# A graph layer on one TensorE: the product of scores and v by one level of Strassen's algorithm

## The chip, the cores and the metric

The kernel runs on one core of one Trainium2 chip. Time is device microseconds of one launch. The median of three runs of the kernel before is 1751.72 us (1751.53 to 1753.11).

## The reference, cut to what matters

64 matrices x of 256 tokens by 512 features go through two layers with one shared 256 by 256 adjacency matrix. All is fp32.

```python
# layer 0
h = relu(layernorm(x))
q, k, v = h @ Wq.T, h @ Wk.T, h @ Wv.T
rel = adj.T * (q @ k.T)                       # 256 x 256 scores, masked
rel = rel / norm(rel, axis=2)                 # each row by its length
x = x + rel @ v                               # <- the product that the change touches
# layer 1
h = relu(layernorm(x))
x = x + (adj @ h) @ weight + bias
```

## The kernel before, in words

The batch is worked in 32 pairs of two matrices (`NB = 2`), each of two token blocks of 128. `x` of five pairs stays in SBUF in a ring (`x_ring`), and each pair's result is added into it in place before it is written out.

For one pair, in steady state, `steady` (L670) issues these stages; each engine runs them in exactly the order in which the Python code issues them, since everything is under `manual_schedule`:

- **attend(i)** (L408): rel times v. Four output tiles of 128 by 512, each two matmuls with 512 moving columns into a PSUM bank of its own; VectorE adds each tile into x, and takes the layer-1 statistics of that tile right after (`side`).
- **project_v(i+1)** (L327): h times Wv.
- **scores(i+1)** (L340): g times h, where g = h times (Wq, Wk folded into one matrix).
- **gather(i)** (L458): adj times h of layer 1, taken in two fp32r parts (upper and lower) when adj is exact in few bits, which it is here (`exact`).
- **project_g(i+2)** (L309): h times the folded matrix.
- **mix(i)** (L481): the gathered rows times weight, added into x.

project_v, scores, project_g and mix already use one level of Strassen's algorithm in Winograd's form. `winograd` (L169) runs seven products instead of eight over three PSUM banks: `bank_a` holds products 1, 6, 7, 4 one on top of the other, `bank_c` products 5 and 3, `bank_b` product 2. After each product a "take" reads the bank and adds it to its quarter of the result. A later product that adds into a bank waits until the take before it has read the bank. In V, scores and g, a take that is the first for its quarter is a copy on ScalarE; the others are adds on VectorE. The first factors of the seven products come from `left_operands` (L152, four sums), the second from `right_operands` (L126, four differences); they are made on VectorE.

`winograd`'s argument `side` is a table from the number of the product (its slot, 0 to 6) to pieces of work that are issued right after that product's take. All other work is placed through it by hand: `norm`'s statistics (`chunk`, L240), its `root` (a small VectorE step and ScalarE's square root) and `end` (reciprocal and bias), the `relus`; for layer 1 `relu_bias` (L439: relu on ScalarE, then the bias added to x by GpSimd), `upper` (a cast on ScalarE) and `lower` (a difference on VectorE). Relus of layer 1 go through two buffers (tag `h2c`), so the third one waits for the first `lower`.

The scores are turned with DMAs (`place`, L376) and four VectorE transposes (`turn`, L383, `turned`), which stand in slot 5 of mix before. The same slot has the end of the layer-0 norm of pair i+4 and its four relus.

Of the kernel before, what the change touches and what calls it, by code (L numbers as in the profile page):

```python
# [19 lines left out]
def kernel(  # L20
# [57 lines left out]
    small = ctx.enter_context(tc.tile_pool(name="small", bufs=3))  # L78
    ps_m = ctx.enter_context(tc.tile_pool(name="ps_m", bufs=8, space=bass.MemoryType.PSUM))

    X, H, HL, G, GS, V, R, H2, Y = ({} for _ in range(9))

    ring = [const.tile([P, NB, NC, D], F32, name=f"x_ring{n}") for n in range(5)]
    blocks = const.tile([P, TC, DC, P], F32, name="blocks")
# [63 lines left out]
    def left_blocks(at):  # L148

        return lambda i, j: at[:, j * HC : (j + 1) * HC, i]  # L150

    def left_operands(pool, at, tag, i):  # L152


        s = pool.tile([P, 3, HC, HT_], F32, tag=tag, name=f"{tag}_{i}")
        a = left_blocks(at)
        v = nc.vector
        steps = [
            lambda: v.tensor_sub(s[:, 0], a(0, 0), a(1, 0)),
            lambda: v.tensor_add(a(1, 0), a(1, 0), a(1, 1)),  # L160
            lambda: v.tensor_sub(s[:, 1], a(1, 0), a(0, 0)),
            lambda: v.tensor_sub(s[:, 2], a(0, 1), s[:, 1]),
        ]
        return (
            {1: a(0, 0), 2: a(0, 1), 3: s[:, 2], 4: a(1, 1), 5: a(1, 0), 6: s[:, 1], 7: s[:, 0]},
            steps,
        )

    def winograd(product, take, side={}, early=False):  # L169

# [138 lines left out]
    def project_g(i, side={}):  # L309

        g = work.tile([P, DC, NC, HT_], F32, tag="g", name=f"g_{i}")

        def take(t, k, bank, first):
            dst = g[:, k * HC : (k + 1) * HC, t, :]
            src = bank.rearrange("p (e t) -> p e t", e=HC)
            if first:
                nc.scalar.copy(dst, src)  # L317
            else:
                nc.vector.tensor_add(dst, src, dst)

        winograd(product_tokens_moving(HL[i], m_right), take, side)
        t = work.tile([P, 3, HC, HT_], F32, tag="gt", name=f"gt_{i}")
        G[i], GS[i] = right_operands(
            lambda j, k: g[:, j * HC : (j + 1) * HC, k], [t[:, n] for n in range(3)]
        )

    def project_v(i, side={}, tag="v"):  # L327
        V[i] = work.tile([P, NB, NC, D], F32, tag=tag, name=f"v_{i}")
# [11 lines left out]
    def scores(i, side={}, by_matmul=False):  # L340


        left, right = HL.pop(i), G.pop(i)
        rel = work.tile([P, NB, NC, N], F32, tag="rel", name=f"rel_{i}")
        placed = work.tile([P, NB, NC, NC, P], F32, tag="placed", name=f"placed_{i}")
        turned = work.tile([P, NB, NC, NC, P], F32, tag="turned", name=f"turned_{i}")
        square = work.tile([P, N], F32, tag="square", name=f"square_{i}")
        rn = small.tile([P, NB, NC], F32, tag="rn", name="rn")
        R[i] = turned

        def take(t, k, bank, first):
            dst = rel[:, :, k, ts(t, P)]
            src = bank[:, :HT_].rearrange("p (b m) -> p b m", b=NB)
            if first:
                nc.scalar.copy(dst, src)
            else:
                nc.vector.tensor_add(dst, src, dst)

        def mask(k):
            nc.vector.tensor_mul(  # L360
                rel[:, :, k], rel[:, :, k], adjt_sb[:, k : k + 1, :].to_broadcast([P, NB, N])
            )

        def square_sum(b, k):
            nc.scalar.activation(square, rel[:, b, k], AF.Square, accum_out=rn[:, b, k : k + 1])

        def root():
            nc.scalar.activation(rn, rn, AF.Sqrt)

        def inverse():  # L370
            nc.vector.reciprocal(rn, rn)

        def scale(b, k):
            nc.scalar.activation(rel[:, b, k], rel[:, b, k], AF.Copy, scale=rn[:, b, k : k + 1])

        def place():  # L376
            rv = rel.rearrange("p b k (t m) -> p (b k t) m", m=P)
            pv = placed.rearrange("p b k t n -> p (b k t) n")
            for j in range(P // S):
                for k in range(P // S):  # L380
                    nc.sync.dma_start(out=pv[ts(j, S), :, ts(k, S)], in_=rv[ts(k, S), :, ts(j, S)])

        def turn(b, k):  # L383
            nc.vector.transpose(turned[:, b, :, k], placed[:, b, k])  # L384

        def each(f):
            return [(lambda b=b, k=k: f(b, k)) for k in range(NC) for b in range(NB)]

        def turn_at_once():
            for b in range(NB):  # L390
                pt = ps_m.tile([P, T], F32, tag="pm", name="pr")
                for t in range(NC):
                    for k in range(NC):
                        nc.tensor.transpose(
                            pt[:, ts(t * NC + k, P)], rel[:, b, k, ts(t, P)], ident
                        )
                nc.scalar.copy(turned[:, b].rearrange("p t k n -> p (t k n)"), pt)

        winograd(product_of_tokens(left, right), take, side)
        if by_matmul:  # L400
            masks = [lambda: mask(0), lambda: mask(1)]
            return masks, each(square_sum), root, inverse, rn, turn_at_once
        return (
            [lambda: mask(0), lambda: mask(1)], each(square_sum), root, inverse, each(scale), place,
            each(turn),
        )

    def attend(i, side={}, scale=None):  # L408
        rel, v, xt = R.pop(i), flat(V.pop(i)), flat(X[i])
        for b in range(NB):  # L410
            for n in range(NC):
                c = b * NC + n
                pm = ps_m.tile([P, 512], F32, tag="pm", name="pu")
                for m in range(NC):
                    nc.tensor.matmul(  # L415
                        pm[:, :D], rel[:, b, m, n], v[:, b * NC + m, :],
                        start=(m == 0), stop=(m == NC - 1),
                    )
                if scale is None:
                    nc.vector.tensor_add(xt[:, c, :], pm[:, :D], xt[:, c, :])  # L420
                else:
                    nc.vector.scalar_tensor_tensor(
                        xt[:, c, :], pm[:, :D], scale[:, b, n : n + 1], xt[:, c, :],
                        op0=ALU.mult, op1=ALU.add,
                    )
                run(side.get(c, ()))


    def ln1(i, exact):
# [179 lines left out]
    def first_pairs(exact):  # L609
# [10 lines left out]
        })  # L620
        place_blocks(1)
        turned1, sums1 = transpose_blocks(1)
        gs = GS.pop(0)
        stats, root, end, relus = ln0(2)
        project_v(0, {
            0: gs[0:2], 1: gs[2:3] + stats[0:1], 2: gs[3:4] + stats[1:2], 3: stats[2:3],
# [11 lines left out]
            4: [inverse] + scales + [place] + stats[3:4] + [root], 5: [end] + w_steps[0:1],  # L638
            6: w_steps[1:4],
        })  # L640
        gs = GS.pop(1)
        turned2, sums2 = transpose_blocks(2)
        project_v(1, {
            0: gs[0:2], 1: gs[2:3] + turned2[0:2], 2: gs[3:4] + turned2[2:4] + relus[0:2],
# [11 lines left out]
        if exact:  # L656
# [1 line left out]
        project_g(2, by_slot(layer_1(parts), {  # L658
            1: [inverse], 3: scales + [place], 4: turned3[0:1], 5: turned3[1:2], 6: turned3[2:4],
        }))  # L660
        y_steps = gather(0, exact, {0: turned3[4:6], 1: turned3[6:7], 2: turned3[7:8]})
        run(y_steps[0:2])
        stats, root, end, relus = ln0(4)
        mix(0, {
            0: y_steps[2:3], 1: y_steps[3:4] + stats[0:1], 2: stats[1:2], 3: stats[2:3],
            4: stats[3:4] + [root], 5: [end] + turns + relus, 6: sums3,
        })
        place_blocks(4)

    def steady(i, exact):  # L670


        stats, root, end, relus, uppers, lowers = ln1(i, exact)
        gs = GS.pop(i + 1)
        attend(i, {c: [stats[c]] for c in range(TC)})
        project_v(i + 1, {
            0: [root, gs[0], end, relus[0], relus[1]],
            1: [uppers[0], uppers[1], gs[1], lowers[0]],
            2: [relus[2], lowers[1]],
            3: [relus[3], uppers[2], uppers[3], gs[2]],  # L680
            4: [lowers[2]],
            5: [lowers[3], gs[3]],
        })
        masks, squares, norm_root, inverse, scales, place, turns = scores(i + 1)
        turned, sums = transpose_blocks(i + 3)
        y_steps = gather(i, exact, {
            0: masks + turned[0:1],
# [1 line left out]
            2: squares[2:4] + turned[3:5],  # L689
            3: [norm_root, inverse] + turned[5:8],  # L690
        })
        project_g(i + 2, {
            0: scales + [place] + y_steps[0:1],
            1: y_steps[1:3],
            2: y_steps[3:4] + sums[0:1],
            3: sums[1:2],
            4: sums[2:3],
            5: sums[3:4],
        })
        if i + 4 < NP:  # L700
            stats, root, end, relus = ln0(i + 4)
            mix(i, {n: [stats[n]] for n in range(TC)} | {4: [root], 5: [end] + turns + relus})
            place_blocks(i + 4)
        else:
            mix(i, {5: turns})

    def last_pairs(exact):

        a, b, c = NP - 3, NP - 2, NP - 1
        stats, *parts = ln1(a, exact)  # L710
        gs = GS.pop(b)
        attend(a, {n: [stats[n]] for n in range(TC)})
        project_v(b, by_slot({0: gs[0:1], 1: gs[1:2], 3: gs[2:3], 5: gs[3:4]}, layer_1(parts)))
        masks, squares, norm_root, inverse, scales, place, turns = scores(b)
        y_steps = gather(a, exact, {
            0: masks, 1: squares[0:2], 2: squares[2:4], 3: [norm_root, inverse],
        })
        project_g(c, {0: scales + [place] + y_steps[0:1], 1: y_steps[1:3], 2: y_steps[3:4]})
        gs = GS.pop(c)
        project_v(c, {  # L720
            0: gs[0:1], 1: gs[1:2], 2: gs[2:3], 3: gs[3:4], 5: turns[0:2], 6: turns[2:4],
        }, tag="h")
# [50 lines left out]
```

## Time and profile before

| | busy us | share of the span |
|---|---|---|
| TensorE, matmuls | 1734.2 | 99% |
| TensorE, weight loads | 1447.8 | 83% |
| VectorE | 1216.7 | 69% |
| ScalarE | 644.6 | 37% |
| GpSimd | 199.4 | 11% |

The span of the profiled execution is 1751.9 us and the granted TensorE clock 0.997. One fp32 matmul appears as two records. A steady pair by stages (from the trace, one pair, us from the span's start):

| stage | from | to | us | VectorE busy | ScalarE busy |
|---|---|---|---|---|---|
| attend | 501.57 | 508.76 | 7.19 | 6.24 | 2.46 |
| V | 508.76 | 521.00 | 12.24 | 10.03 | 6.75 |
| scores | 521.00 | 527.25 | 6.25 | 2.26 | 1.70 |
| gather | 527.25 | 530.90 | 3.65 | 2.96 | 2.55 |
| g | 530.90 | 542.98 | 12.08 | 8.28 | 5.12 |
| mix | 542.98 | 555.07 | 12.09 | 7.94 | 1.27 |

How to read it: TensorE's busy time fills the span, so a stage's length is the length of its matmuls plus the moments in which TensorE waits. The last columns say how full the engines beside it are in that stage. Records of matmuls overlap at their ends, so lengths are taken from the start of one group to the start of the next.

### The profile page before, as it was taken

To read this page: it belongs to the slowest core of one execution; us is meant where nothing else is said; L and a number is where in the kernel's file an instruction comes from. 1 tells how busy PE (TensorE), PEld (TensorE's weight loads), DVE (VectorE), ACT (ScalarE), POOL (GpSimd) and SP (SyncE) were. 2 spreads that over 40 slices of the span, in tenths; PEclk is the share of its full clock that TensorE was granted. 3 is DMA by queue.
4 is the path that set the end of the run, shared out by engine and by line. 5 is a ranking of instruction groups with operands and counts; after the bars stand their busy time and mean duration, and the time that the engine had idled before them with its cause. 6 is when DMAs were issued, how large, how long until landed. Compare 5 with 4: busy or idle time off the path is not lost.

```text
span 1751.9 us, 23847 instructions
## 1 busy us (share of the span) xinstructions
PE 1734.2 (99%) x8822; PEld 1447.8 (83%) x8822; DVE 1216.7 (69%) x2353; ACT 644.6 (37%) x1387; POOL 199.4 (11%) x167
## 2 busy tenths in 40 slices
PE   8999999999999999999999999999999999999998
PEld 7978887888888888878888888888788888888886
DVE  6776777666777667776667776677766677766555
ACT  3433433334423334333344233343333442333332
POOL 0011111011110011110111100111101111001111
PEclk9999999999999999999999999999999999999999
DMA  6423333223332233332233422333322333222101
GB/s 232 64 44 70 77 80 71 58 53 84 74 85 55 51 76 76 81 68 61 53 83 74 85 56 52 74 78 80 74 57 52 83 75 85 53 55 50 30 13 69
DMA packets 425966, 122.27 MB, mean 70 GB/s; under 512 B 398064, under 2 KB 399344, under 8 KB 425840
## 3 DMA queue, kind: packets, MB, share of 16 engines
q1 hardware_dynamic: 413248, 80.28, 24.9%
q0 software_dynamic: 8432, 32.51, 5.2%
q10 hardware_dynamic: 4160, 7.87, 1.3%
q8 instruction: 71, 1.16, 0.3%
q14 instruction: 55, 0.45, 0.1%
HBM read 38.27 MB, written 33.55 MB: 41 GB/s over the span
## 4 chain that ended last, share of the span: by engine, by line
PE 95%; DVE 3%; ACT 0%; DMA 0%; issue 0%; ACTq 0%; DVEq 0%
PE bank_a L210 25%; PE bank_a L198 12%; PE bank_c L210 12%; PE pu L415 12%; PE py L470 7%; PE bank_a L222 7%; PE bank_b L210 6%; PE bank_c L198 6%; PE bank_c L222 3%; PE bank_b L198 3%; PE bank_b L222 2%; DVE st L241 1%; DMA wk_sb<-in_L_gnn_Wk_dram 0%; DVE x_ring L420 0%; DVE x_ring L487 0%
## 5 line engine op out<-in xcount | busy, mean ns | idle before, releaser
L415 PE MATMUL pu<-v,turned 128*128 128x512 f32 x512 | 227.1, 596 | 3.2 <-DVE turned L384 0.9
L443 POOL TENSOR_TENSOR x_ring<-x_ring,bias_bc 128x512 f32<-128x512 f32 x128 | 174.6, 1383 | 452.1 <-ACT h2c L253 452.1
L415 PEld LDWEIGHTS pu<-v,turned 128*128 128x128 f32 x512 | 94.7, 190 | 120.8 <-issue 107.2
L241 DVE BATCH_NORM_STATS2 st<-x_ring 128x6 f32<-128x512 f32 x256 | 176.2, 688 | 4.4
L334 ACT COPY v<-bank_a 128x512 f32<-128x512 f32 x96 | 56.0, 583 | 308.3 <-PE bank_a L210 300.9
L451 DVE TENSOR_TENSOR h<-h2c,h 128x512 fp32r<-128x512 f32 x128 | 123.2, 980 | 62.9 <-ACT h L447 62.9
L494 POOL DMA_DIRECT2D out_dram<-x_ring x31 | 24.0, 773 | 1080.3 <-issue 796.7
L487 DVE TENSOR_TENSOR x_ring<-bank_a,x_ring 128x512 f32<-128x512 f32 x128 | 87.3, 682 | 80.3 <-PE bank_a L210 76.4
L317 ACT COPY g<-bank_a 128x512 f32<-128x512 f32 x96 | 56.2, 585 | 213.7 <-PE bank_a L198 213.5
L470 PE MATMUL py<-adjt_r,h 128*128 128x256 f32 x1024 | 124.9, 280 | 0.0
L210 PE MATMUL bank_a<-w_t,ys 128*128 128x256 f32 x512 | 121.3, 380 | 1.8 <-DVE x_ring L487 1.8
L210 PE MATMUL bank_a<-wv_t,hs 128*128 128x256 f32 x512 | 121.0, 379 | 0.0
L198 PE MATMUL bank_a<-hs,m_t 128*128 128x256 f32 x512 | 120.9, 379 | 0.0
L470 PEld LDWEIGHTS py<-adjt_r,h 128*128 128x128 f32 x1024 | 119.4, 188 | 0.1
L246 ACT ACTIVATE rs<-rs 128x4 f32<-128x4 f32 x64 | 13.2, 206 | 268.2 <-DVE rs L245 268.2
L210 PEld LDWEIGHTS bank_a<-w_t,ys 128*128 128x128 f32 x512 | 96.9, 190 | 16.2 <-DVE x_ring L487 3.0
L253 ACT ACTIVATE h<-x_ring,nb,rs 128x512 f32<-128x512 f32 x124 | 90.9, 802 | 50.3 <-DVE nb L250 50.3
L253 ACT ACTIVATE h2c<-x_ring,nb,rs 128x512 f32<-128x512 f32 x128 | 97.4, 807 | 30.9 <-DVE h L451 16.4
L198 PEld LDWEIGHTS bank_a<-hs,m_t 128*128 128x128 f32 x512 | 97.3, 190 | 13.2
L210 PEld LDWEIGHTS bank_a<-wv_t,hs 128*128 128x128 f32 x512 | 97.3, 190 | 13.2
L420 DVE TENSOR_TENSOR x_ring<-pu,x_ring 128x512 f32<-128x512 f32 x124 | 85.6, 690 | 27.3 <-PE pu L415 20.4
L302 DVE STREAM_TRANSPOSE ht<-blocks 128x256 f32<-128x256 f32 x248 | 87.2, 408 | 1.1 <-DMA blocks<-h 1.1
(152 smaller groups left out, 3235.3 us busy)
## 6 DMA issues: line engine op xcount, KB each, us to landing
blocks<-h SPq DMA_DIRECT2D x496, 64.0 KB, 2.3
out_dram<-x_ring POOLq DMA_DIRECT2D x31, 1024.0 KB, 5.2
x_ring<-in_x_dram SPq DMA_DIRECT2D x28, 1024.0 KB, 5.6
placed<-rel SPq DMA_DIRECT2D x496, 32.0 KB, 2.0
x_ring<-in_x_dram ACTq DMA_DIRECT2D x4, 1024.0 KB, 5.4
wq_sb<-in_L_gnn_Wq_dram SPq DMA_DIRECT2D x4, 256.0 KB, 5.1
wk_sb<-in_L_gnn_Wk_dram ACTq DMA_DIRECT2D x4, 256.0 KB, 6.9
wv_sb<-in_L_gnn_Wv_dram ACTq DMA_DIRECT2D x1, 1024.0 KB, 5.4
```

The source lines that it names most:

```text
L198: nc.tensor.matmul(bank[:, e * HT_ : (e + 1) * HT_], right[n][:, d, ts(e, P)], left[n][:, d, :], start=(start and e == 0 and d == 0), stop ...
L210: nc.tensor.matmul(bank[:, b * HD : (b + 1) * HD], left[n][:, d, ts(b, P)], right[n][:, d, :], start=(start and b == 0 and d == 0), stop=( ...
L222: nc.tensor.matmul(bank[:, ts(b, P)], right[n][:, d, ts(b, P)], left[n][:, d, ts(b, P)], start=(start and b == 0 and d == 0), stop=(d == H ...
L241: nc.vector.bn_stats(st[:, c, :], src[:, c, :])
L253: nc.scalar.activation(dst, src[:, c, :], AF.Relu, bias=nb[:, c : c + 1], scale=rs[:, c : c + 1])
L302: nc.vector.transpose(ht[:, d, half].rearrange("p (b n) -> p b n", b=NB), by_half[:, :, half, d])
L415: nc.tensor.matmul(pm[:, :D], rel[:, b, m, n], v[:, b * NC + m, :], start=(m == 0), stop=(m == NC - 1),)
L420: nc.vector.tensor_add(xt[:, c, :], pm[:, :D], xt[:, c, :])
L443: nc.gpsimd.tensor_tensor(xt[:, c, :], xt[:, c, :], bias_bc, ALU.add)
L451: nc.vector.tensor_sub(dst[:, 1, c, :], whole_h[c], dst[:, 0, c, :].bitcast(F32))
L470: nc.tensor.matmul(pm[:, d, :], left[:, b * NC + m, ts(d0 + d, P)], right, start=(n == 0), stop=(n == len(terms) - 1),)
L487: nc.vector.tensor_add(xt[block], bank.rearrange("p (b e) -> p b e", b=NB), xt[block])
```

## The change

In pairs 1 to 29 the product of the normed scores and v is done by seven half-size products instead of eight, to cut TensorE's work. Pairs 0, 30 and 31 keep the plain product.

Per product there are now two matmuls of 256 moving columns, one for each matrix of the pair. The left factors are made in place from `turned`, with the dead `rel` tile for the new sums; the right ones from `v` and a new tile under the tag of g's factors (`gt`). So g's differences are only prepared after attend (`g_operands`), and v's in project_g, slots 4 to 6. The turns move from slot 5 to slot 4 of mix, and the four sums of the turned scores (`rel_steps`) go into slot 5. Each take of the new product is an add into x on VectorE. A quarter of x is finished only at the end of the product, so the statistics of layer 1 move from attend into slots 0 and 1 of V, and what follows from them (root, end, relus, upper and lower parts) moves back by some slots, the last two lower parts into scores. In the first pair the sums for pair 3 still stand in slot 6 of mix.

```diff
+    def attend_operands(i):
+        turned, rel = R.pop(i)
+        v, t = V.pop(i), work.tile([P, 3, NB, HD], F32, tag="gt", name=f"vt_{i}")
+        room = rel.rearrange("p b k m -> p (b k m)")
+        left, left_steps = left_factors(
+            lambda n, m: turned[:, :, m, n],
+            [room[:, ts(j, HT_)].rearrange("p (b n) -> p b n", b=NB) for j in range(3)],
+        )
+        right, right_steps = right_operands(
+            lambda m, k: v[:, :, m, ts(k, HD)], [t[:, n] for n in range(3)]
+        )
+        R[i] = left, right
+        return right_steps, left_steps
+
+    def attend_by_strassen(i):
+        xt, (left, right) = X[i], R.pop(i)
+        def product(bank, n, start):
+            for b in range(NB):
+                nc.tensor.matmul(
+                    bank[:, ts(b, HD)], left[n][:, b], right[n][:, b],
+                    start=(start and b == 0), stop=True, skip_group_check=True,
+                )
+        def take(t, k, bank, first):
+            dst = xt[:, :, t, ts(k, HD)]
+            nc.vector.tensor_add(dst, bank.rearrange("p (b e) -> p b e", b=NB), dst)
+        winograd(product, take)
...
     def steady(i, exact):
-        stats, root, end, relus, uppers, lowers = ln1(i, exact)
-        gs = GS.pop(i + 1)
-        attend(i, {c: [stats[c]] for c in range(TC)})
-        project_v(i + 1, {
-            0: [root, gs[0], end, relus[0], relus[1]],
-            1: [uppers[0], uppers[1], gs[1], lowers[0]],
-            2: [relus[2], lowers[1]],
-            3: [relus[3], uppers[2], uppers[3], gs[2]],
-            4: [lowers[2]],
-            5: [lowers[3], gs[3]],
-        })
-        masks, squares, norm_root, inverse, scales, place, turns = scores(i + 1)
+        attend_by_strassen(i)
+        stats, *parts = ln1(i, exact)
+        gs = g_operands(i + 1)
+        project_v(i + 1, v_side(stats, gs, *parts))
+        masks, squares, norm_root, inverse, scales, place, turns = scores(i + 1, s_side(*parts))
...
         project_g(i + 2, {
...
-            4: sums[2:3],
-            5: sums[3:4],
+            4: sums[2:3] + v_steps[0:1],
+            5: sums[3:4] + v_steps[1:2],
+            6: v_steps[2:4],
         })
         if i + 4 < NP:
             stats, root, end, relus = ln0(i + 4)
-            mix(i, {n: [stats[n]] for n in range(TC)} | {4: [root], 5: [end] + turns + relus})
+            mix(i, {n: [stats[n]] for n in range(TC)} | {
+                4: [root] + turns, 5: [end] + rel_steps + relus,
+            })
...
+    def v_side(stats, gs, root, end, relus, uppers, lowers):
+        halves = [stats[b * NC + t] for t in range(NC) for b in range(NB)]
+        return {
+            0: halves[0:2],
+            1: halves[2:4] + [root],
+            2: [end, relus[0], relus[1]] + gs[0:2],
+            3: [uppers[0], uppers[1]] + gs[2:3],
+            4: [lowers[0], relus[2], lowers[1], relus[3]],
+            5: gs[3:4],
+            6: [uppers[2], uppers[3]],
+        }
+
+    def s_side(root, end, relus, uppers, lowers):
+        return {0: [lowers[2]], 1: [lowers[3]]}
```

More of the change, by code (lines that the diff above doesn't have):

```diff
@@ L79 @@
     ps_m = ctx.enter_context(tc.tile_pool(name="ps_m", bufs=8, space=bass.MemoryType.PSUM))
-    X, H, HL, G, GS, V, R, H2, Y = ({} for _ in range(9))
+    X, H, HL, G, V, R, H2, Y = ({} for _ in range(8))
     ring = [const.tile([P, NB, NC, D], F32, name=f"x_ring{n}") for n in range(5)]
@@ L150, in left_blocks, with left_factors @@
         return lambda i, j: at[:, j * HC : (j + 1) * HC, i]
+    def left_factors(a, s):
+        v = nc.vector
+        steps = [
+            lambda: v.tensor_sub(s[0], a(0, 0), a(1, 0)),
+            lambda: v.tensor_add(a(1, 0), a(1, 0), a(1, 1)),
+            lambda: v.tensor_sub(s[1], a(1, 0), a(0, 0)),
+            lambda: v.tensor_sub(s[2], a(0, 1), s[1]),
+        ]
+        return {1: a(0, 0), 2: a(0, 1), 3: s[2], 4: a(1, 1), 5: a(1, 0), 6: s[1], 7: s[0]}, steps
     def left_operands(pool, at, tag, i):
         s = pool.tile([P, 3, HC, HT_], F32, tag=tag, name=f"{tag}_{i}")
[L156 to L167, printed above, removed]
+        return left_factors(left_blocks(at), [s[:, n] for n in range(3)])
     def winograd(product, take, side={}, early=False):
@@ L321, in project_g, with g_operands @@
         winograd(product_tokens_moving(HL[i], m_right), take, side)
-        t = work.tile([P, 3, HC, HT_], F32, tag="gt", name=f"gt_{i}")
-        G[i], GS[i] = right_operands(
+        G[i] = g
+    def g_operands(i):
+        g, t = G[i], work.tile([P, 3, HC, HT_], F32, tag="gt", name=f"gt_{i}")
+        G[i], steps = right_operands(
             lambda j, k: g[:, j * HC : (j + 1) * HC, k], [t[:, n] for n in range(3)]
         )
+        return steps
     def project_v(i, side={}, tag="v"):
@@ L348, in scores @@
         rn = small.tile([P, NB, NC], F32, tag="rn", name="rn")
-        R[i] = turned
+        R[i] = turned, rel
         def take(t, k, bank, first):
@@ L408, in attend @@
     def attend(i, side={}, scale=None):
-        rel, v, xt = R.pop(i), flat(V.pop(i)), flat(X[i])
+        rel, v, xt = R.pop(i)[0], flat(V.pop(i)), flat(X[i])
         for b in range(NB):
@@ L622, in first_pairs @@
         turned1, sums1 = transpose_blocks(1)
-        gs = GS.pop(0)
+        gs = g_operands(0)
         stats, root, end, relus = ln0(2)
@@ L640, in first_pairs @@
         })
-        gs = GS.pop(1)
+        gs = g_operands(1)
         turned2, sums2 = transpose_blocks(2)
@@ L660, in first_pairs @@
         }))
-        y_steps = gather(0, exact, {0: turned3[4:6], 1: turned3[6:7], 2: turned3[7:8]})
+        v_steps, rel_steps = attend_operands(1)
+        y_steps = gather(0, exact, {
+            0: turned3[4:8], 1: v_steps[0:1], 2: v_steps[1:3], 3: v_steps[3:4],
+        })
         run(y_steps[0:2])
@@ L665, in first_pairs @@
             0: y_steps[2:3], 1: y_steps[3:4] + stats[0:1], 2: stats[1:2], 3: stats[2:3],
-            4: stats[3:4] + [root], 5: [end] + turns + relus, 6: sums3,
+            4: stats[3:4] + [root] + turns, 5: [end] + rel_steps + relus, 6: sums3,
         })
@@ L691, in steady @@
         })
+        v_steps, rel_steps = attend_operands(i + 1)
         project_g(i + 2, {
@@ L701, in steady @@
             stats, root, end, relus = ln0(i + 4)
-            mix(i, {n: [stats[n]] for n in range(TC)} | {4: [root], 5: [end] + turns + relus})
+            mix(i, {n: [stats[n]] for n in range(TC)} | {
+                4: [root] + turns, 5: [end] + rel_steps + relus,
+            })
             place_blocks(i + 4)
         else:
-            mix(i, {5: turns})
+            mix(i, {4: turns, 5: rel_steps})
+    def v_side(stats, gs, root, end, relus, uppers, lowers):
[11 more added lines that the diff above has]
+        return {0: [lowers[2]], 1: [lowers[3]]}
     def last_pairs(exact):
         a, b, c = NP - 3, NP - 2, NP - 1
+        attend_by_strassen(a)
         stats, *parts = ln1(a, exact)
[L711 to L714, printed above, removed]
+        gs = g_operands(b)
+        project_v(b, v_side(stats, gs, *parts))
+        masks, squares, norm_root, inverse, scales, place, turns = scores(b, s_side(*parts))
         y_steps = gather(a, exact, {
@@ L718, in last_pairs @@
         project_g(c, {0: scales + [place] + y_steps[0:1], 1: y_steps[1:3], 2: y_steps[3:4]})
-        gs = GS.pop(c)
+        gs = g_operands(c)
         project_v(c, {
```

## The prediction

> **What bounds the kernel now.** I read the page's shares and chain first, then one steady pair on each engine's timeline.
>
> ```profile
> PE 1734.2 (99%) x8822; PEld 1447.8 (83%) x8822; DVE 1216.7 (69%) x2353; ACT 644.6 (37%) x1387; POOL 199.4 (11%) x167
> PE 95%; DVE 3%; ACT 0%; DMA 0%; issue 0%; ACTq 0%; DVEq 0%
> ```
>
> TensorE is the chain, so a matmul saved counts unless TensorE then waits. Its timeline (start, length, count):
>
> ```profile
> 499.84 1.89 PE L210 MATMUL bank_a<-w_t,yt 128*128 128x256 f32 x8
> 501.82 7.11 PE L415 MATMUL pu<-v,turned 128*128 128x512 f32 x16
> 508.76 1.89 PE L210 MATMUL bank_a<-wvt_sb,ht 128*128 128x256 f32 x8
> ...
> 517.42 1.89 PE L210 MATMUL bank_b<-wvt_sb,ht 128*128 128x256 f32 x8
> 519.17 1.99 PE L210 MATMUL bank_a<-wv_t,ht 128*128 128x256 f32 x8
> 521.00 1.05 PE L222 MATMUL bank_a<-ht,g 128*128 128x128 f32 x8
> 521.89 1.06 PE L222 MATMUL bank_c<-ht,g 128*128 128x128 f32 x8
> ```
>
> I measure from start to start. Eight 256-wide records take 1.73 us (0.216 each), eight 128-wide 0.89. The last mix product would end at 499.84 + 1.73 = 501.57; V starts at 508.76. So the attend stage costs 7.19 us: 6.94 of matmuls and 0.25 of waiting for the turned scores. V takes 12.24 where seven times 1.73 is 12.10.
>
> What a wait costs is shown where TensorE does stall:
>
> ```profile
> 1697.17 1.89 PE L210 MATMUL bank_c<-w_sb,ys 128*128 128x256 f32 x8
> 1699.45 1.99 PE L210 MATMUL bank_a<-w_t,ys 128*128 128x256 f32 x8 [0.39 <-DVE x_ring L487]
> 1701.28 1.89 PE L210 MATMUL bank_b<-w_sb,yt 128*128 128x256 f32 x8
> ```
>
> ```profile
> 1698.71 0.68 DVE L487 TENSOR_TENSOR x_ring<-bank_a,x_ring 128x512 f32<-128x512 f32 x1
> ```
>
> The take (the read of the bank) ends at 1699.39, the waiting product starts 0.06 later, and the next product comes after 1.83 instead of 1.73: a stall costs 0.10 on top. The same 1.83 stands between 519.17 and 521.00 above.
>
> VectorE at the end of a mix, where the change puts its work:
>
> ```profile
> 498.31 0.69 DVE L487 TENSOR_TENSOR x_ring<-bank_a,x_ring 128x512 f32<-128x512 f32 x1 [0.22 <-PE bank_a L210]
> 498.92 0.16 DVE L245 TENSOR_SCALAR rs<-mv 128x4 f32<-128x4 f32 x1
> 500.04 0.69 DVE L487 TENSOR_TENSOR x_ring<-bank_b,x_ring 128x512 f32<-128x512 f32 x1 [0.96 <-PE bank_b L210]
> ...
> 501.22 1.42 DVE L384 STREAM_TRANSPOSE turned<-placed 128x256 f32<-128x256 f32 x4 [0.21 <-issue]
> 502.57 0.65 DVE L487 TENSOR_TENSOR x_ring<-bank_a,x_ring 128x512 f32<-128x512 f32 x1
> ```
>
> The take of the last mix product, ready about 501.77, already comes 0.8 us late. Nobody minds: each 512-wide attend product has a bank of its own. ScalarE's queue in V and scores:
>
> ```profile
> 513.24 0.56 ACT L334 COPY v<-bank_c 128x512 f32<-128x512 f32 x1
> 513.71 1.14 ACT L447 CAST h<-h2c 128x512 fp32r<-128x512 f32 x2
> 514.75 0.58 ACT L334 COPY v<-bank_a 128x512 f32<-128x512 f32 x1
> ...
> 521.20 0.58 ACT L334 COPY v<-bank_a 128x512 f32<-128x512 f32 x1 [2.85 <-PE bank_a L210]
> 522.09 0.37 ACT L355 COPY rel<-bank_a 128x256 f32<-128x256 f32 x1 [0.31 <-PE bank_a L222]
> ```
>
> A copy holds the queue 0.47 us before casts, two casts 1.04, and a copy starts 0.20 after its product's end. The casts are over long before the copy at 521.20.
>
> [...] a product that adds into a bank waits for its take; the stall above is one. [...] the third g difference takes 1.63 us while the bias is added, a take from PSUM then 0.68.
>
> **The change, part by part.** Products are P1, P5, P6, P3, P7, P2, P4 in order of issue; P1, P6, P7, P4 share bank_a, P5 and P3 bank_c. 29 pairs change (1 to 29).
>
> (1) Matmuls. Sixteen 512-wide records become 28 of 256. 28 x 0.216 = 6.05 us, against 7.19: a gain of 1.14 if nothing waits. Turning earlier removes the 0.25.
>
> (2) Return of a bank. Take 0.20 after the product's end, 0.69 long, then 0.06: 0.95 us. Only one product of 0.865 lies between. P7 and P4 each stall 0.085 + 0.10 = 0.185, 0.37 together. In mix the product between is 1.73 and hides this.
>
> (3) VectorE's queue ahead of P1's take. From the take of mix's P7 at 498.31, in order: take P7 0.61, root 0.2, four turns 1.42, take P2 0.61, reciprocal and bias 0.3, four sums of 256 columns, take P4 0.61, P1's take 0.69. The trace has no 256-wide sum from SBUF; [...] 0.46 with the 0.04 seen between dependent sums: 1.72 with the overlap at the end. Bounds: 0.34 each (spacing of the 256-column transposes), 1.36; or 0.55, 2.2. Sum 6.16, so P1's take ends at 504.47. TensorE reaches P6 at 501.57 + 2 x 0.865 = 503.30. Stall 504.53 - 503.30 + 0.10 = 1.33 (bounds 0.75 to 1.7). P5 waits for the second sum, ready about 502.35, before its 502.43. The stage: 6.05 + 1.33 + 0.37 = 7.75, 0.56 worse than before.
>
> (4) Three more takes and four v factors (0.69 to 0.73 each). The v factors lie in the end of project_g, where VectorE sat idle 0.4, 0.4 and 2.2 us (before 486.23, 487.95 and 491.48); counted through, that take comes at 544.84 to 544.91, when ready anyhow. Cost nothing.
>
> (5) Statistics of layer 1 in V. From V's start: take of P4 to 0.93, four chunks of about 0.85 to 4.3, root, ScalarE's root and inverse to 5.3. The first two relus follow the copy of P6, 5.9 to 7.4, casts to 8.4. The bias (GpSimd) slows the third g difference to 1.63, until 9.3; take of P7 to 9.9, lower parts at 9.9 and 10.5, second relus 10.6 to 12.15. V's last copy is ready at 12.31. Behind it in ScalarE's queue stand two casts, then the copy of scores' P1: 12.31 + 0.47 + 1.04 = 13.82, ends 14.19. Scores' P6 wants that bank at 12.11 + 2 x 0.893 = 13.90: stall 14.25 - 13.90 + 0.10 = 0.45. If the chain is late by more than 0.15, it grows one for one; the bounds are 0.3 and 0.8. Before, the copy at 522.09 ended 0.3 early. Against it, V's own 0.14 of stalls goes, since VectorE has only a v take and a g step there.
>
> (6) First pair: mix 0 has four more 0.7 us sums behind its last take, ahead of P1's take of pair 1; counted through, its P6 stalls about 5.0 instead of 1.33: +3.7 once. Pair 29 has no root and bias in front: -0.5.
>
> Sum: per pair +0.56 + 0.45 - 0.14 = +0.87; 29 x 0.87 + 3.2 = 28.4. So 1751.7 + 28.4 = 1780.
>
> **Rivals.** (a) Only the VectorE queue bites; ScalarE's casts slip past the P1 copy: 29 x 0.42 + 3.2 = 15.4, 1767. Against: the order of the queue is fixed. (b) The bias contention makes the relu chain 0.4 later: 29 x 1.27 + 3.2, 1792. For: two g steps now lie near the biases. (c) The end of mix absorbs turns and sums, and only the bank return remains: 6.05 + 0.55 = 6.60, -0.59 - 0.14 = -0.73 a pair, 1731: faster. For: VectorE is 69% busy, and rises by 29 x 6.5 us (eight sums, three takes) to about 1406, still under the span. Against: the 6.16 of (3) stand in 5.19 us of TensorE's time. (d) No wait at all: 29 x (1.14 + 0.14) = 37 saved, 1715.
>
> **How the numbers follow.** The forecast 0.56, (a) 0.17, (b) 0.12, (c) 0.08, (d) 0.02, and 0.05 for stalls and savings that cancel. The point is the forecast's. Both stalls at their low bounds give 29 x 0.14 + 3 = 7, both high 29 x 1.59 + 3 = 49; with some of the corners left out, 1756 to 1796. Faster 0.10, same 0.05, slower 0.85.
>
> **What would show it.** Right: in attend TensorE waits on VectorE before P6 for over 1 us and shortly before P7 and P4; in scores it waits about 0.4 on ScalarE's copy; a pair takes 54.4 instead of 53.5. Wrong: P1's take starting within 0.3 of its product, or the scores copy ahead of the casts.

## The result, and the profile after

The changed kernel takes 1775.2 us (median of four runs, 1774.21 to 1775.73) against 1752.3 us before: 22.9 us more, a ratio of 1.013 with a 95% interval of 1.0112 to 1.0148. 1780 was forecast, within 1756 to 1796.

The page's shares, and the first line of the chain, of the changed kernel:

```profile
PE 1726.1 (97%) x9170; PEld 1516.5 (86%) x9170; DVE 1371.2 (77%) x2672; ACT 645.4 (36%) x1387; POOL 213.0 (12%) x167
PE 83%; DVE 11%; ACT 3%; issue 2%; DMA 1%; DVEq 0%; ACTq 0%
```

TensorE does less, as intended (1726 us busy in place of 1734), in a longer span. Part of the waiting is hidden in this busy time: the same 9170 records are busy for 1699.6 us in the last kernel of this document, where TensorE hardly waits. The chain now runs 11% through VectorE and 3% through ScalarE: there are stages in which TensorE waits. The list of waits names them (who waited for whom, us in total, times, longest):

```profile
PE bank_a L454 <- DVE x_ring L461: 25.0, 29, 3.8
PE bank_a L222 <- ACT rel L360: 5.9, 29, 0.2
```

L454 is the new product and L461 its take; L222 is a product of scores and L360 its copy. One steady pair by stages, in us between the starts of groups:

| stage | before | after | difference |
|---|---|---|---|
| attend | 7.19 | 7.46 | +0.27 |
| V | 12.24 | 12.08 | -0.16 |
| scores | 6.25 | 6.72 | +0.47 |
| gather | 3.65 | 3.66 | +0.01 |
| g | 12.08 | 12.08 | 0 |
| mix | 12.09 | 12.09 | 0 |
| pair | 53.50 | 54.09 | +0.59 |

The pair follows, first TensorE's timeline in attend (start, length, count; in brackets the wait and what ended it):

```profile
562.70 1.03 PE L454 MATMUL bank_a<-v,turned 128*128 128x256 f32 x4
563.56 1.03 PE L454 MATMUL bank_c<-v,turned 128*128 128x256 f32 x4
565.36 1.13 PE L454 MATMUL bank_a<-vt,rel 128*128 128x256 f32 x4 [0.77 <-DVE x_ring L461]
566.33 1.03 PE L454 MATMUL bank_c<-v,rel 128*128 128x256 f32 x4
567.27 1.13 PE L454 MATMUL bank_a<-vt,rel 128*128 128x256 f32 x4
568.24 1.03 PE L454 MATMUL bank_b<-v,turned 128*128 128x256 f32 x4
569.19 1.13 PE L454 MATMUL bank_a<-vt,turned 128*128 128x256 f32 x4
```

and the first products of scores, one pair earlier:

```profile
528.93 1.06 PE L222 MATMUL bank_c<-ht,g 128*128 128x128 f32 x8
530.19 1.16 PE L222 MATMUL bank_a<-hs,gt 128*128 128x128 f32 x8 [0.20 <-ACT rel L360]
531.18 1.06 PE L222 MATMUL bank_c<-hs,g 128*128 128x128 f32 x8
```

P5 starts at 563.56 and would end at 564.43, but P6 starts at 565.36, 0.93 later, and the next product follows after 0.97 instead of 0.865: 1.03 us lost. P7 and P4 start 0.95 instead of 0.865 after the product ahead of them, and again lose 0.10 on top: 0.18 each. In scores P6 starts 0.37 late and also loses 0.10. The page's bracket shows less than the whole loss: it counts from the end of the record ahead, 564.59, which is 0.16 past 564.43.

VectorE at the same end of mix:

```profile
559.45 0.69 DVE L524 TENSOR_TENSOR x_ring<-bank_a,x_ring 128x512 f32<-128x512 f32 x1 [0.22 <-PE bank_a L210]
560.05 0.16 DVE L245 TENSOR_SCALAR rs<-mv 128x4 f32<-128x4 f32 x1
560.12 1.42 DVE L389 STREAM_TRANSPOSE turned<-placed 128x256 f32<-128x256 f32 x4
...
563.68 0.43 DVE L161 TENSOR_TENSOR rel<-turned,rel 128x256 f32<-128x256 f32 x1
564.02 0.68 DVE L524 TENSOR_TENSOR x_ring<-bank_a,x_ring 128x512 f32<-128x512 f32 x1
564.63 0.68 DVE L461 TENSOR_TENSOR x_ring<-bank_a,x_ring 128x512 f32<-128x512 f32 x1
```

It works without a gap from the take of mix's P7 (559.45) to P1's take, which ends at 565.31; P6 starts 0.05 later. ScalarE at the end of V:

```profile
582.44 0.59 ACT L339 COPY v<-bank_a 128x512 f32<-128x512 f32 x1 [0.46 <-PE bank_a L210]
582.93 1.14 ACT L484 CAST h<-h2c 128x512 fp32r<-128x512 f32 x2
583.97 0.38 ACT L360 COPY rel<-bank_a 128x256 f32<-128x256 f32 x1
```

V ends at 582.24 on TensorE; its copy, two casts, and then the copy of scores' P1, which P6 needs, ends at 584.35.

Not all is in the steady pairs. In pair 1 attend takes 12.98 us:

```profile
124.39 1.03 PE L454 MATMUL bank_a<-v,turned 128*128 128x256 f32 x4
126.18 1.13 PE L454 MATMUL bank_c<-v,turned 128*128 128x256 f32 x4 [0.76 <-DVE turned L159]
131.08 1.60 PE L454 MATMUL bank_a<-vt,rel 128*128 128x256 f32 x4 [3.77 <-DVE x_ring L461]
132.47 1.91 PE L454 MATMUL bank_c<-v,rel 128*128 128x256 f32 x4
134.18 1.44 PE L454 MATMUL bank_a<-vt,rel 128*128 128x256 f32 x4
```

P5 waits 0.92 for the second sum, P6 3.9 for P1's take, and the three products from P6 on then take 1.39, 1.71 and 1.28 us. The table of stretches gives the granted clock (the first number after the busy times of the five engines):

```profile
131.08:132.47 1.39, 1.39 (x4) 1.16 (x5) 0.54 (x1) 0.00 (x0) 0.00 (x0) 0.69 1.04 410
132.47:134.18 1.71, 1.71 (x5) 1.35 (x4) 0.69 (x1) 0.00 (x0) 0.00 (x0) 0.50 0.93 243
134.18:135.46 1.28, 1.28 (x5) 1.05 (x4) 0.69 (x1) 0.00 (x0) 0.00 (x0) 0.68 0.95 124
```

It fell to 0.5 to 0.7 behind the long wait. The first mix also waits 1.4 us for a sum of the gathered rows, since v's factors of pair 1 now stand ahead of it in VectorE's queue, and on the other side V of pair 2 loses a wait of 1.2 us on ScalarE that it had before. By stages, 28 x 0.27 for attend, 5.8 for pair 1's (12.98 - 7.19), 29 x 0.31 for V and scores, 1.6 for the first mix and a further -1.4 for V of pair 2 make 22.5 of the 22.9 us. (In the two profiled executions the spans differ by 20.3 only: near the start the third product of the first matrix begins at 12.04 after and at 14.62 before. There TensorE waited for weights until 8.81 instead of 7.91, and the granted clock behind that wait was 0.50 and 0.55 where it is 1.00 after.)

### The profile page after: what moved, and what is told of

Same layout as the page of the kernel before. It is cut to its first block, busy times and chain, and to the rows that moved or that the text cites. A ratio compares the mean times of both kernels' runs of the same rounds, so it can differ in the third digit from the quotient of the medians.

```text
span 1772.2 us, 24834 instructions
## 1 busy us (share of the span) xinstructions
PE 1726.1 (97%) x9170; PEld 1516.5 (86%) x9170; DVE 1371.2 (77%) x2672; ACT 645.4 (36%) x1387; POOL 213.0 (12%) x167
## 4 chain that ended last, share of the span: by engine, by line
PE 83%; DVE 11%; ACT 3%; issue 2%; DMA 1%; DVEq 0%; ACTq 0%
PE bank_a L210 22%; PE bank_c L210 12%; PE bank_a L198 12%; PE py L507 6%; PE bank_c L198 6%; PE bank_a L222 5%; PE bank_a L454 5%; PE bank_b L210 3%; PE bank_b L198 3%; DVE x_ring L524 2%; DVE turned L389 2%; ACT h L484 2%; PE bank_c L222 2%; PE bank_b L222 2%; PE bank_c L454 1%
## 5 line engine op out<-in xcount | busy, mean ns | idle before, releaser
L480 POOL TENSOR_TENSOR x_ring<-x_ring,bias_bc 128x512 f32<-128x512 f32 x128 | 188.0, 1489 | 527.4 <-ACT h2c L253 527.4
L488 DVE TENSOR_TENSOR h<-h2c,h 128x512 fp32r<-128x512 f32 x128 | 107.7, 876 | 17.5 <-ACT h L484 17.5
L461 DVE TENSOR_TENSOR x_ring<-bank_a,x_ring 128x512 f32<-128x512 f32 x116 | 80.0, 690 | 39.6 <-PE bank_a L454 39.6
L524 DVE TENSOR_TENSOR x_ring<-bank_a,x_ring 128x512 f32<-128x512 f32 x128 | 88.2, 689 | 19.7 <-PE bank_a L210 12.9
L454 PE MATMUL bank_a<-vt,rel 128*128 128x256 f32 x232 | 66.4, 409 | 25.0 <-DVE x_ring L461 25.0
L511 ACT COPY yt<-py 128x512 f32<-128x512 f32 x128 | 74.0, 578 | 32.9 <-PE py L507 32.9
```

What stands on the lines that cost most here:

```text
L454: nc.tensor.matmul(bank[:, ts(b, HD)], left[n][:, b], right[n][:, b], start=(start and b == 0), stop=True, skip_group_check=True,)
L461: nc.vector.tensor_add(dst, bank.rearrange("p (b e) -> p b e", b=NB), dst)
L480: nc.gpsimd.tensor_tensor(xt[:, c, :], xt[:, c, :], bias_bc, ALU.add)
L488: nc.vector.tensor_sub(dst[:, 1, c, :], whole_h[c], dst[:, 0, c, :].bitcast(F32))
L524: nc.vector.tensor_add(xt[block], bank.rearrange("p (b e) -> p b e", b=NB), xt[block])
```

## The experiments

The theory is that of the prediction: the saved matmuls are there, but the new product brings three waits: on VectorE's queue at the end of mix, on ScalarE's queue between V and scores, and on the return of a bank when only one short product lies between. The rivals: the later statistics alone are the loss; VectorE's larger total load is; P6 waits for the sums of the turned scores and not for a take. The runs below come from several sessions, in which the kernel before took 1752.3 to 1753.6 us; each ratio is to the kernel before of its own session, and differences between two experiments are good to about 1 us.

### One part alone: the statistics in V, with the plain product

```diff
 # before.py, steady (last_pairs in the same way)
...
-        attend(i, {c: [stats[c]] for c in range(TC)})
-        project_v(i + 1, {
-            0: [root, gs[0], end, relus[0], relus[1]],
...
-        })
-        masks, squares, norm_root, inverse, scales, place, turns = scores(i + 1)
+        attend(i)
+        project_v(i + 1, v_side(stats, gs, *parts))
+        masks, squares, norm_root, inverse, scales, place, turns = scores(i + 1, s_side(*parts))
```

> The kernel before with one part of the change alone: the statistics of layer 1 and what follows from them in V and scores, the plain product of eight kept. Queue theory: scores stall 0.46 us a pair on the copy behind the casts (29 pairs, 13.3 us), V's own stalls of 0.14 go (-4), so about 9 us slower than before, 1761. Rival that the Strassen product itself is the whole loss: no change, 1752. Rival that the later statistics are the whole loss: 1775, as the changed kernel.

Measured: 1761.6 us, ratio to before 1.005 (1.0033 to 1.0067), 8.6 us slower. Its list of TensorE's waits:

```profile
PE bank_a L222 <- ACT rel L355: 5.9, 29, 0.2
```

That is the line of the changed kernel, to the tenth, with the plain product in attend. V takes 12.08, as there. So the wait in scores belongs to the moved statistics, and it is 8.6 of the 22.9 us: the later statistics are neither nothing nor all of it.

### One cast moved: the wait on ScalarE's queue

```diff
-            4: [lowers[0], relus[2], lowers[1], relus[3]],
+            4: [lowers[0], relus[2], uppers[2], lowers[1], relus[3]],
...
-            6: [uppers[2], uppers[3]],
+            6: [uppers[3]],
```

> The changed kernel with the third upper cast moved from slot 6 to slot 4 of V, right behind its relu, so that only one cast stands between V's last copy and scores' first. Queue theory: the copy comes 0.5 us earlier, the wait of 0.46 in scores goes in 29 pairs: 13 us less than the changed kernel, 1762; attend keeps its 7.46. Rival that the relu chain itself is late: ScalarE only idles earlier and nothing moves, 1775.

Measured: 1762.5 us, ratio to before 1.0055 (1.0038 to 1.0071), 12.7 less than the changed kernel. ScalarE between V and scores, and TensorE:

```profile
579.11 0.56 ACT L339 COPY v<-bank_a 128x512 f32<-128x512 f32 x1
579.58 0.62 ACT L484 CAST h<-h2c 128x512 fp32r<-128x512 f32 x1
580.10 0.37 ACT L360 COPY rel<-bank_a 128x256 f32<-128x256 f32 x1
```

```profile
579.70 1.06 PE L222 MATMUL bank_c<-ht,g 128*128 128x128 f32 x8
580.59 1.08 PE L222 MATMUL bank_a<-hs,gt 128*128 128x128 f32 x8
581.51 1.06 PE L222 MATMUL bank_c<-hs,g 128*128 128x128 f32 x8
```

The copy now ends at 580.47, before P6's turn at 580.59, and P6 is followed after 0.92 where it was 0.99 and 0.37 late. One cast out of the way is worth 12.7 us, and attend keeps its waits (25.0 us in the list, unchanged).

### The same work, spread: the wait on VectorE's queue

```diff
+        chunks = []
+        if i + 4 < NP:
+            chunks, root, end, relus = ln0(i + 4)
         y_steps = gather(i, exact, {
...
-            2: squares[2:4] + turned[3:5],
+            2: squares[2:4] + turned[3:5] + chunks[0:2],
...
-            mix(i, {n: [stats[n]] for n in range(TC)} | {
-                4: [root] + turns, 5: [end] + rel_steps + relus,
+            mix(i, {
+                0: chunks[2:3], 1: chunks[3:4], 2: [root], 3: [end] + turns + relus,
+                4: rel_steps[0:2], 5: rel_steps[2:4],
             })
...
```

> The changed kernel with VectorE's work at the end of mix spread: two statistics of the layer-0 norm into gather, root to slot 2, end, turns and relus to slot 3, the sums of the turned scores two each in slots 4 and 5. Same work, other places. Queue theory: P1's take comes on time, the wait before P6 shrinks from 1.04 to the 0.18 of a bank return, attend from 7.46 to about 6.6: 28 x 0.86 = 24 us less than the changed kernel, 1751. Rival that VectorE's total load or the small products are the cause: the wait stays, 1775.

Measured: 1754.4 us, ratio to before 1.0005 (0.9996 to 1.0013), 20.8 less than the changed kernel. TensorE and VectorE around the start of attend:

```profile
558.99 1.03 PE L454 MATMUL bank_c<-v,turned 128*128 128x256 f32 x4
559.94 1.13 PE L454 MATMUL bank_a<-vt,rel 128*128 128x256 f32 x4
560.90 1.03 PE L454 MATMUL bank_c<-v,rel 128*128 128x256 f32 x4
```

```profile
558.34 0.68 DVE L524 TENSOR_TENSOR x_ring<-bank_a,x_ring 128x512 f32<-128x512 f32 x1
559.19 0.69 DVE L461 TENSOR_TENSOR x_ring<-bank_a,x_ring 128x512 f32<-128x512 f32 x1 [0.17 <-PE bank_a L454]
```

P1's take now waits for its product, and what is left before P6 is the return of the bank, as before P7 and P4: the stage takes 6.60. The work on VectorE is the same (1373 us busy, against 1371), so its total is not the cause. The gain is 20.8 and not 24, mainly because the turns in slot 3 make one take of mix late: mix's last product is followed after 1.82 instead of 1.73, 0.10 a pair. Another 0.7 is pair 1's attend, which this edit doesn't touch: it took 13.67 us in place of 12.98, with slower products behind the same wait of 3.77.

### One idle add in the queue

```diff
-                4: [root] + turns, 5: [end] + rel_steps + relus,
+                4: [root] + turns, 5: [end] + rel_steps + [one_more] + relus,
...
+    def one_more():
+        nc.vector.tensor_add(scratch, w_sb[:, 0], w_sb[:, 1])
```

> The changed kernel with one idle VectorE add of 512 columns (a scratch tile nobody reads) behind the four sums of the turned scores, ahead of the take of mix's P4, in 27 mixes. Queue theory: P1's take comes later by what an add holds the queue, 0.61 us, and the wait before P6 grows by that: 27 x 0.61 = 16.5, 1792. Rival that P6 waits for the sums of the turned scores and not for P1's take: the sums are done before the add, no change, 1775.

Measured: 1792.1 us, ratio to before 1.0218 (1.0201 to 1.0235), 16.9 more than the changed kernel.

```profile
568.95 0.43 DVE L162 TENSOR_TENSOR rel<-turned,rel 128x256 f32<-128x256 f32 x1
569.29 0.69 DVE L746 TENSOR_TENSOR scratch<-w_sb 128x512 f32<-128x512 f32 x1
569.89 0.68 DVE L525 TENSOR_TENSOR x_ring<-bank_a,x_ring 128x512 f32<-128x512 f32 x1
570.49 0.68 DVE L462 TENSOR_TENSOR x_ring<-bank_a,x_ring 128x512 f32<-128x512 f32 x1
```

```profile
568.83 1.03 PE L455 MATMUL bank_c<-v,turned 128*128 128x256 f32 x4
571.23 1.13 PE L455 MATMUL bank_a<-vt,rel 128*128 128x256 f32 x4 [1.37 <-DVE x_ring L462]
```

(All lines stand one lower in this file; the second fence has P5 and P6.) The add holds the queue 0.60 us, and the bracket grows from 0.77 to 1.37; over the whole run the list of waits has 41.3 us for this line instead of 25.0. The sums were done before it, so P6 waits for P1's take. What stands there costs one for one.

### Both moves together

> The two moves together. Queue theory: two separate waits, so the gains add: 13 + 24 = 37 us less than the changed kernel, 1738, faster than the kernel before. Rival that the waits hide each other (one taken away, the other grows): about as the better one of the two alone, 1751 or more.

Measured: 1740.9 us, ratio to before 0.9931 (0.9914 to 0.9948), 34.3 less than the changed kernel, where the two alone gave 12.7 + 20.8 = 33.5. The waits are separate and add. The kernel is now faster than before.

### Another order and a fourth bank

```diff
-        winograd(product, take)
...
+        for bank, n, start, blocks_of_x in [
+            (bank_a, 1, True, [(0, 0)]),
+            (bank_c, 5, True, [(1, 1)]),
+            (bank_b, 2, True, [(0, 0)]),
+            (bank_a, 6, False, [(0, 1)]),
+            (bank_c, 3, False, [(0, 1)]),
+            (bank_d, 4, True, [(1, 0)]),
+            (bank_a, 7, False, [(1, 1), (1, 0)]),
+        ]:
+            product(bank, n, start)
+            for t, k in blocks_of_x:
+                take(t, k, bank, False)
```

> The changed kernel with only the order and the banks of the new product changed: P1, P5, P2, P6, P3, P4, P7, where P4 has a bank of its own, and the sum P1+P6+P7 is added to both lower quarters (one take more, eight in all). Nothing is moved in mix. Bank-return theory: two products lie between every product and the next one into its bank (1.73 us against the 0.95 of a return), and P6 is reached at 3 x 0.865 after the start, when P1's take (2.61 after the start in the trace) is just over. All waits of attend go: 7.46 to about 6.1, 29 x 1.36 = 39 us less than the changed kernel, 1736. Rival that VectorE's load decides (it gets 0.61 us a pair more): slower than the changed kernel, about 1790.

Measured: 1739.6 us, ratio to before 0.9922 (0.9907 to 0.9937), 35.6 less than the changed kernel, although VectorE has one take more per pair.

```profile
503.16 1.03 PE L454 MATMUL bank_b<-v,turned 128*128 128x256 f32 x4
504.09 1.13 PE L454 MATMUL bank_a<-vt,rel 128*128 128x256 f32 x4
505.06 1.03 PE L454 MATMUL bank_c<-v,rel 128*128 128x256 f32 x4
```

P6 comes one product later and P1's take is just too late for it: 0.07 and the 0.10 of a stall are left. In attend nothing waits after that. The stage takes 6.22 instead of 7.46. This undoes more than the whole loss without moving a single piece of side work, and it speaks once more against the total load. It doesn't tell the return of a bank from the queue, since the new order also gives P1's take one product more of time; the pair of kernels under "All of it" does.

### The first pair

The kernel with both moves; in the first pair the sums for pair 3 go to V and scores of the next step, v's factors over gather and mix, and the norm statistics of pair 4 into project_g; the turns are split over slots 2 and 3 of mix.

```diff
         project_g(2, by_slot(layer_1(parts), {
-            1: [inverse], 3: scales + [place], 4: turned3[0:1], 5: turned3[1:2], 6: turned3[2:4],
+            1: [inverse], 3: scales + [place], 4: turned3[0:1], 5: turned3[1:2] + stats4[0:2],
+            6: turned3[2:4] + stats4[2:4],
         }))
...
-            0: turned3[4:8], 1: v_steps[0:1], 2: v_steps[1:3], 3: v_steps[3:4],
...
+        y_steps = gather(0, exact, {0: turned3[4:8], 1: v_steps[0:1]})
...
         mix(0, {
-            0: y_steps[2:3], 1: y_steps[3:4] + stats[0:1], 2: stats[1:2], 3: stats[2:3],
-            4: stats[3:4] + [root] + turns, 5: [end] + rel_steps + relus, 6: sums3,
+            0: y_steps[2:3], 1: y_steps[3:4] + v_steps[1:2], 2: v_steps[2:3] + [root4],
+            3: [end4] + v_steps[3:4] + turns[0:2] + relus4, 4: turns[2:4] + rel_steps[0:2],
+            5: rel_steps[2:4],
         })
...
```

> The kernel with both moves, and besides: the turns split over slots 2 and 3 of mix, and in the first pair the sums for pair 3 out of slot 6 of mix into V and scores of the next step, v's factors of pair 1 spread over gather and mix, the norm statistics of pair 4 in project_g. Queue theory: mix's own 0.10 a pair goes (28 x 0.10 = 3), attend of pair 1 from 13.0 to about 6.6 us and the first mix's wait of 1.5 goes: together 10 to 11 less than the kernel with both moves, 1730. If the first pair's waits only move to another stage: 1738.

Measured: 1736.0 us, ratio to before 0.99 (0.9885 to 0.9915), only 4.9 less than with both moves. Attend of pair 1 came to 6.89 us, but the first mix from 13.7 to 16.5:

```profile
114.70 3.02 PE L210 MATMUL bank_c<-w_sb,yt 128*128 128x256 f32 x8 [2.47 <-DVE yt L159]
117.50 2.57 PE L210 MATMUL bank_a<-w_t,ys 128*128 128x256 f32 x8
119.91 1.89 PE L210 MATMUL bank_c<-w_sb,ys 128*128 128x256 f32 x8
```

The statistics that I put into project_g hold up VectorE there, the sums of the gathered rows come later still, and behind the wait of 2.5 us two products take 2.80 and 2.41 us (granted clock 0.64 and 0.72). Pair 1's attend gained 6.7 us (13.63 with both moves), and 2.8 of them came back in the first mix.

### All of it

The kernel of the last section with the order and the fourth bank of the section before it.

> All of it together: early cast, early norm, first pair, and the new order with four banks. Bank-return theory: the three returns of 0.18 a pair go as well, 29 x 0.55 = 16 us less than the kernel before this one: 1715, close to the 1751.7 - 37 that the saved matmuls and V's stalls allow. Rival that returns cost nothing once VectorE is on time: 1730.

Measured: 1718.1 us, ratio to before 0.9798 (0.9784 to 0.9811): 17.9 less than the same kernel with three banks. A steady attend takes 6.05 instead of 6.61, so the returns cost 0.56 a pair even when VectorE is on time, 16 us in all. The other 1.7 us are in the first mix, which took 14.8 instead of 16.5 although its wait is the same:

```profile
115.38 1.97 PE L210 MATMUL bank_c<-w_sb,yt 128*128 128x256 f32 x8 [2.46 <-DVE yt L159]
117.18 1.89 PE L210 MATMUL bank_a<-w_t,ys 128*128 128x256 f32 x8
```

Behind this wait of 2.5 us the two products take 1.80 and 1.73 us, not 2.80 and 2.41; the changed kernel's two at this place take 1.80 and 1.72 at a granted clock of 1.00.

Last, the first pair placed anew:

```diff
         project_v(1, {
...
-            3: turned2[4:6] + relus[2:4], 4: turned2[6:8], 5: turns[0:2], 6: turns[2:4],
+            3: turned2[4:6] + relus[2:4], 4: turned2[6:8], 5: stats4[0:2] + turns[0:2],
+            6: turns[2:4],
         })
...
-            0: sums2[0:1], 1: sums2[1:2], 2: sums2[2:3], 6: sums2[3:4],
+            0: sums2[0:1], 1: sums2[1:2], 2: sums2[2:3], 6: sums2[3:4] + stats4[2:4],
...
-        y_steps = gather(0, exact, {0: turned3[4:8], 1: v_steps[0:1]})
+        y_steps = gather(0, exact, {0: turned3[4:8]})
...
-            0: y_steps[2:3], 1: y_steps[3:4] + v_steps[1:2], 2: v_steps[2:3] + [root4],
-            3: [end4] + v_steps[3:4] + turns[0:2] + relus4, 4: turns[2:4] + rel_steps[0:2],
-            5: rel_steps[2:4],
+            0: y_steps[2:3], 1: y_steps[3:4] + v_steps[0:1], 2: v_steps[1:2] + [root4],
+            3: [end4] + v_steps[2:3] + turns[0:2] + relus4,
+            4: v_steps[3:4] + turns[2:4] + rel_steps[0:1], 5: rel_steps[1:4],
```

> All three moves with the first pair placed anew: the four norm statistics of pair 4 in the two places of V(1) and scores(1) where VectorE sat idle 1.5 and 1.6 us, and v's factors of pair 1 out of gather into slots 1 to 4 of mix. Queue theory: the wait of 2.5 us before the second product of mix 0, and the slow products after it (2.80 and 2.41 instead of 1.73), go: 4 us less, 1714. If the wait only moves again: 1717 to 1719.

Measured: 1714.3 us, ratio to before 0.9776 (0.9759 to 0.9792). The wait in the first mix is gone (12.09 us for the stage); the slow products behind it, which the expectation counted too, were not in the profile of the kernel just before this one. The stretch of one attend stage, and the page's shares:

```profile
542.39:548.44 6.05, 6.05 (x30) 5.32 (x29) 4.82 (x7) 0.00 (x0) 0.77 (x1) 1.00 0.70 192
```

```profile
PE 1699.6 (99%) x9170; PEld 1521.4 (89%) x9170; DVE 1407.4 (82%) x2701; ACT 648.1 (38%) x1387; POOL 210.1 (12%) x167
```

The stage takes the 6.05 us that 28 records of 0.216 need. VectorE is busier than in the changed kernel (1407 us against 1371) in a span that is 60 us shorter.

## Why the prediction was right

- **Step 1, the matmuls** (6.05 in place of 7.19): right; the last kernel shows 6.05 us. The 0.25 of waiting for the turned scores went as well.
- **Step 2, the return of a bank** (0.185 before P7 and P4): right, 0.18 each in the trace. That it costs on its own was shown by the fourth bank in a kernel whose VectorE is on time: 0.56 a pair for three returns, 16 us over 29 pairs.
- **Step 3, VectorE's queue** (stall of 1.33 before P6): the mechanism was right, the size too high; 1.03 was measured. From mix's P7 to the end of P1's take the queue took 5.86 us and not 6.16. The mis-sized terms are the root, which holds the queue for 0.07 (from 560.05 to 560.12) where 0.2 was put in, and the four turns, 1.34 from start to start (560.12 to 561.46) where their length of 1.42 was put in, though the trace of before already had 1.35 (501.22 to 502.57); the other terms were each up to 0.03 too high. The 1.72 for the four sums was the author's estimate, and held: they take 1.71 from the start of the first to that of the next take (562.31 to 564.02), 0.42 to 0.43 each, as long as a 256-wide take of scores before (0.42 at 524.84), and 0.46 from one dependent sum to the next. The stated bounds of 0.75 to 1.7 don't follow from those of the sums: 1.36 and 2.2 in place of 1.72 give 0.97 and 1.81, and the 2.2 was a margin from no trace. The sign "over 1 us before P6" is met only with the 0.10 of the restart: P6 itself was 0.93 late.
- **Step 4, v's factors at nothing**: right in the steady pairs, where the first mix take comes when its product is done and mix keeps its 12.09. Wrong in the first pair, where they stand in gather ahead of the sums of the gathered rows: 1.6 us once.
- **Step 5, the statistics in V** (0.45 in scores, V 0.14 shorter): right, 0.47 and 0.16. The chain of relus was expected 0.15 ahead of V's last copy and came 0.45 ahead (581.99 against 582.44). One link of its working was wrong: the third g difference was to be slowed to 1.63 by the bias and took 0.80, though the first two bias adds ran beside it (576.92 to 579.87), and the fourth took 1.62 beside the other two (581.36 to 584.31), behind the first lower parts and so without delaying the second relus. That this part costs 8.6 us by itself was shown by running it alone.
- **Step 6, the first pair** (+3.7 over a steady one): too low, +5.5. P5 and P6 together waited 5.0 (0.9, a restart of 0.10, and 3.9), as much as was counted for P6 alone. But a steady P6 loses 1.03 and not 1.33, and the products from P6 to P7 took 4.38 us where a steady pair has 2.88: the slower clock added 1.5 that no step had. Pair 29 gained 0.36 over a steady one (7.10), where 0.5 was counted.
- **The rivals.** Case (a), the casts slipping past, did not come (casts from 582.93, the copy at 583.97), and neither did (b): the relu chain was earlier than counted; (c) is not how the change as it stands behaves, but its number for attend, 6.60, is what the kernel with the spread work reached. (d), no wait at all, was put at 1715 and is what the last kernel reaches, 1714, after four edits.

Summed, +0.59 a pair was measured against +0.87; the difference is step 3 almost alone (0.30). Over 29 pairs that is 8 us too much. What comes only once was counted about 2.5 us too low, so the total, 5.5 us too high, is in part nearer than its terms by luck.

## What to carry to other kernels

A product that is cut into smaller pieces must be checked for the time between two uses of a bank: here 0.95 us from a product's end to the restart, which products of 1.73 us hid and products of 0.865 did not. Ask of every piece of side work what stands behind it in its engine's queue, and who waits for that: the same VectorE work in other slots was worth 21 us, one cast 13, and an idle add cost its full 0.60 us each time, while VectorE was only 77% busy. When a change saves matmuls and the kernel gets slower, list TensorE's waits by line first; here that list named both queues at once. It did not show the return of a bank, whose 0.18 us each time is too short for its brackets.

## What the runs showed that had not been expected

- After the wait of 3.8 us in pair 1 (waits here are those of the brackets) the granted clock was 0.69, 0.50 and 0.68 over the next 4.4 us in the changed kernel, and 0.50 and 0.50 over the next 3.6 us behind the same wait in the kernel with both moves, whose two products there took 1.87 and 1.71 us; with the idle add two took the same 1.87 and 1.71. After a wait of 2.9 us, with the new order alone, two took 1.87 and 1.41 us, where at a granted clock of 1.00 a steady pair has 0.97 behind a stall (565.36 to 566.33) and 0.865 without one. After a wait of 2.5 us in the first mix the granted clock was 0.64 and 0.72 over 5.2 us in one kernel, while in another the products took the 1.80 and 1.73 us told above, and after one of 1.4 us it stayed at 1.00. So waits of 2.9 and 2.5 us were followed by slow products too, though not every time. What decides it is not shown.
- A stall of 0.02 us (519.17 before) and one of 0.93 us (565.36 after) each cost TensorE 0.10 us on top, at a granted clock of 1.00, so four small waits cost more than one long one of the same sum.
- The four turns followed 0.21 us of "issue" when they came behind two short instructions (501.22 before), and none when they came behind a take and the short root (560.12 after). Why is not shown.
